# Token routing and parts of the expert layer issued between the edge batches of a graph-attention and mixture-of-experts kernel

## The chip, the cores and the metric

The kernel runs on one NeuronCore of a Trainium2 chip. The metric is the device time of one execution in microseconds (us), the median of several runs. The names in this text: PE is the matrix engine (TensorE), PEld its weight loads, DVE the vector engine, ACT the scalar engine, POOL is GpSimd, SP is SyncE, which only waits and issues DMAs. "L833" is line 833 of the kernel before.

## The reference

6,250 nodes with 256 features, 100,000 edges sorted by destination. The destinations are skewed towards low node numbers: the first 128 nodes have 14,487 of the edges. A graph-attention layer is followed by a layer of 8 experts, both residual:

```python
# graph part, on layernorm(x); 4 heads of 64 features
messages = h_fwd[src] * direction[:, 0:1] + h_rev[src] * direction[:, 1:2]
scores = leaky_relu(einsum('ef,hf->eh', messages, attn[0]), 0.2)
exp_scores = exp(scores - scores.max(axis=0, keepdims=True))
norm = exp_scores / (segment_sum(exp_scores, dst)[dst] + 1e-10)
outs = [segment_sum(messages * norm[:, hd:hd + 1], dst) for hd in range(4)]
# expert part, on layernorm(x + outs); C = ceil(1.25 * T / 8) rows per expert
idx = argmax(softmax(x @ gate_w + gate_b)); prb = that probability
pos = (cumsum(one_hot(idx), axis=0) * one_hot).sum(-1) - 1
kept = pos < C
buf = zeros((E, C, D)).at[idx, pos].set(x, mode='drop')
ybuf = relu(buf @ w1 + b1) @ w2 + b2
y = ybuf[idx, min(pos, C - 1)] * (prb * kept)
```

Everything is float32. The expert layer's hidden width is 1,024.

## The kernel before

`tile_gnn_ffn_kernel` (from L519) works in five stages, each in its own scope of buffers, one after another. (`general_path` above it computes the same for any input; it runs at the end, at L1113, only if a flag `bad_i` says that the assumptions of the fast path do not hold.)

1. **Node table** (L667 to L698). The 49 tiles of 128 nodes, in 7 chunks, are normalised and multiplied by both weight matrices; the table of 136 values per node goes to DRAM as `node_tab`. Then the edge lists are loaded and transposed (L703 to L739), and DVE derives for each group of 768 edges (`GT` = 6 tiles of 128) the first destination and the place of each edge in the group's window of 128 nodes (`local`, L751). SP also writes zeros to `buf` (L793).
2. **Edges** (L811 to L912): 131 groups in 66 batches of two. Per batch: POOL issues 12 indirect gathers from `node_tab` into `gt`, which has four buffers (L831 to L835). DVE forms the messages `m` (L841 to L848), the scores (L851 to L859); ACT takes the exponential (L863); DVE forms the products `v` (L865) and the one-hot matrix `hot` (L870). PE sums each group over its edges into `pv` (L876) and adds the sum carried over from the group before with a matrix `zt` (L885). ACT copies `pv` to `r` (L887, four buffers) and SP stores it into `sums` at a row read from a register (L888 to L890). `m`, `v` and `hot` have three buffers.
3. **Routing** (L946 to L1027): 7 chunks of 7 tiles. `sums` is read back, divided and added to x, normalised, transposed on PE, multiplied by the gate (L966); some 25 small DVE operations turn the gate's values into a slot per token; POOL scatters each tile's rows into `buf` (L1021).
4. **Experts** (L1032 to L1086): for each of the 8 experts the weights are loaded on SP (two buffers), up to 977 rows come on ACT's queue in eight pieces and are transposed (L1058), multiplied with `w1` (L1068), passed through ReLU (L1070), multiplied with `w2` (L1077); DVE adds the bias and SP stores to `ybuf` (L1086).
5. **Combining** (L1091 to L1107): POOL gathers each token's row of `ybuf` (L1097, four buffers), ACT scales it (L1100), DVE clamps and adds, SP stores.

Each engine works its instructions in its queue's order. In the kernel before a scheduler puts the instructions of one scope in order. A later stage starts when what it reads is complete: the routing reads `sums` that the last edge group has written, the experts read `buf` that the last token may have entered, the combining reads `ybuf`.

Of the kernel before, what the change touches and what calls it, by code (L numbers as in the profile page):

```python
# [8 lines left out]
F32 = mybir.dt.float32  # L9
# [5 lines left out]
P = 128  # L15
# [504 lines left out]
def kernel(  # L520
# [24 lines left out]

    nc = tc.nc
# [23 lines left out]
    CHAIN = 16  # L570
    SPREAD = 40.0
    TROWS = N + P - 1
    NSLOT = E * CAP
# [5 lines left out]
    sums = dram.tile([TROWS, ACC], F32, name="sums")  # L579
    buf = dram.tile([NSLOT + NT * P, D], F32, name="buf")  # L580
# [39 lines left out]
    def load_nodes(t, c):  # L620

        r0 = c * CH * P
        if c < NCK - 1:
            nc.sync.dma_start(t, x[r0:r0 + CH * P, :].rearrange("(n p) d -> p n d", p=P))
            return
        nc.vector.memset(t[96:P, CH - 1, :], 0.0)
        r1 = (NT - 1) * P
        nc.sync.dma_start(t[:, :CH - 1, :], x[r0:r1, :].rearrange("(n p) d -> p n d", p=P))
        nc.sync.dma_start(t[:LAST, CH - 1, :], x[r1:N, :])

    def store_nodes(to, t, c):
        r0 = c * CH * P
        if c < NCK - 1:
            nc.sync.dma_start(to[r0:r0 + CH * P, :].rearrange("(n p) d -> p n d", p=P), t)
            return
        r1 = (NT - 1) * P
        nc.sync.dma_start(to[r0:r1, :].rearrange("(n p) d -> p n d", p=P), t[:, :CH - 1, :])
        nc.sync.dma_start(to[r1:N, :], t[:LAST, CH - 1, :])

    def layernorm(pool, h, t):  # L640

        st = pool.tile([P, CH, nc.vector.BN_STATS_DIM], F32, name="ln_st")
        mv = pool.tile([P, CH, nc.vector.BN_AGGR_DIM], F32, name="ln_mv")
        for n in range(CH):
            nc.vector.bn_stats(st[:, n, :], t[:, n, :])
            nc.vector.bn_aggr(mv[:, n, :], st[:, n, :])
        sd = pool.tile([P, CH], F32, name="ln_sd")
        nc.scalar.activation(sd, mv[:, :, 1], AF.Sqrt, bias=eps_t)
        rs = pool.tile([P, CH], F32, name="ln_rs")
        nc.vector.reciprocal(rs, sd)  # L650
        for n in range(CH):
            nc.vector.tensor_scalar(h[:, n, :], t[:, n, :], mv[:, n, 0:1], rs[:, n:n + 1],  # L652
                                    op0=OP.subtract, op1=OP.mult)
# [13 lines left out]
    with tc.tile_pool(name="p1", bufs=2) as p1, \  # L667
# [18 lines left out]
        for c in range(NCK):  # L686
            xt = p1.tile([P, CH, D], F32, name="xt", bufs=3)
            load_nodes(xt, c)
            h = p1.tile([P, CH, D], F32, name="h")
            layernorm(p1, h, xt)  # L690
# [7 lines left out]
            store_nodes(node_tab, nt, c)  # L698
# [8 lines left out]
    dstf = ep.tile([P, EW], F32, name="dstf")  # L707
    ea = ep.tile([P, 2, EW], F32, name="ea")
    with tc.tile_pool(name="pi", bufs=1) as pi, \
# [32 lines left out]
    starts = ep.tile([P, NG + 1], F32, name="starts")  # L742
# [8 lines left out]
    local = ep.tile([P, ET], F32, name="local")  # L751
# [6 lines left out]
    high = ep.tile([P, NG], F32, name="high")  # L758
    nc.vector.tensor_sub(high, starts[:, 1:NG + 1], begin)
    carry_from = ep.tile([P, NG], F32, name="carry_from")  # L760
# [3 lines left out]
    nc.vector.tensor_tensor(carry_from[:, CHAIN:GF], last_tile[:, CHAIN:GF], high[:, CHAIN:GF], OP.is_equal)  # L764

    base_f = ep.tile([1, NG], F32, name="base_f")
    nc.vector.tensor_scalar(base_f, begin[0:1, :], 0.0, float(N - 1), op0=OP.max, op1=OP.min)
    base_i = ep.tile([1, NG], I32, name="base_i")
# [4 lines left out]
    wrong = ep.tile([P, 5], F32, name="wrong")  # L773
    t0 = ep.tile([P, ET], F32, name="t0")
# [13 lines left out]
    nc.vector.memset(wrong[:, 4:5], 1.0)  # L788
    nc.vector.tensor_sub(t0[0:1, CHAIN:GF], high[0:1, CHAIN:GF], last_tile[0:1, CHAIN:GF])
    nc.vector.tensor_reduce(wrong[0:1, 4:5], t0[0:1, CHAIN:GF], AX.X, OP.min)  # L790
    nc.vector.tensor_scalar(wrong[:, 4:5], wrong[:, 4:5], 0.0, None, op0=OP.is_le)

    for r in range(0, NSLOT, 512):  # L793
        k = min(512, NSLOT - r)
        nc.sync.dma_start(buf[r:r + k, :].rearrange("(p n) d -> p (n d)", n=4), zeros[:k // 4, :])

    nc.sync.dma_start(sums[N:TROWS, :], zeros[0:TROWS - N, 0:ACC])


    batches = [list(range(g, min(g + 2, NG))) for g in range(0, NG, 2)]  # L800
    GB = 2 * GT
    gmax = ep.tile([P, len(batches), H], F32, name="gmax")
    shift = ep.tile([P, H], F32, name="shift")
    ZN = 8
# [4 lines left out]


    with tc.tile_pool(name="p2", bufs=3) as p2, \  # L811
            tc.tile_pool(name="ps2", bufs=6, space=bass.MemoryType.PSUM) as ps2:


        fixed = ps2.tile([P, P + H + 2 * (2 + H) * GB], F32, name="fixed", bufs=1)
        nc.vector.tensor_copy(fixed[:, 0:P], lane)
        lane_p, shift_p = fixed[:, 0:P], fixed[:, P:P + H]
        turns = fixed[:, P + H:].rearrange("p (t k j) -> p t k j", t=2, j=GB)

        def over_partitions(to, t):  # L820

            pm = ps2.tile([P, H, P], F32, name="pm", tag="pv")
            for hd in range(H):
                nc.tensor.transpose(pm[:, hd, :], t[:, hd:hd + 1].to_broadcast([P, P]), ident)
            nc.vector.tensor_reduce(to, pm, AX.X, OP.max)

        before = None
        for b, gs in enumerate(batches):
            i0, i1 = gs[0] * GT, min((gs[-1] + 1) * GT, ET)
            n = i1 - i0  # L830
            gt = p2.tile([P, GB, ROW], F32, name="gt", bufs=4)  # L831
            for i in range(i0, i1):
                nc.gpsimd.indirect_dma_start(  # L833
                    out=gt[:, i - i0, :], out_offset=None, in_=node_tab,
                    in_offset=bass.IndirectOffsetOnAxis(ap=srci[:, i:i + 1], axis=0))  # L835
            m = p2.tile([P, GB, MS], F32, name="m")

            fac = turns[:, b % 2, 0:2, :]
# [3 lines left out]
            for g in gs:  # L842
                a0, a1 = g * GT - i0, min((g + 1) * GT, ET) - i0
                k = a1 - a0
                rv = ps2.tile([P, GT, MS], F32, name="rv", bufs=1)
# [10 lines left out]
            if b == 0:  # L856
# [4 lines left out]
            w = fixed[:, P + H + (b % 2 * (2 + H) + 2) * GB:P + H + (b % 2 + 1) * (2 + H) * GB]  # L861
            w = w.rearrange("p (j h) -> p j h", h=H)
            nc.scalar.activation(v[:, :n, H * O:ACC], s, AF.Exp)  # L863
            nc.vector.tensor_copy(w[:, :n, :], v[:, :n, H * O:ACC])  # L864
# [4 lines left out]
            hot = p2.tile([P, GB, P], F32, name="hot")  # L869
            nc.vector.tensor_tensor(hot[:, :n, :], lane_p.unsqueeze(1).to_broadcast([P, n, P]),  # L870
                                    local[:, i0:i1].unsqueeze(2).to_broadcast([P, n, P]), OP.is_equal)
            for g in gs:
                tiles = list(range(g * GT, min((g + 1) * GT, ET)))
                pv = ps2.tile([P, ACC], F32, name="pv")
                for i in tiles:
                    nc.tensor.matmul(pv, hot[:, i - i0, :], v[:, i - i0, :], start=(i == tiles[0]),  # L876
                                     stop=(i == tiles[-1] and before is None))
                if before is not None:
                    k = (g - 1) % ZN
                    z = zt[(g - 1) // ZN % 2]  # L880
                    if k == 0:
                        nz = min(ZN, NG - g)

                        nc.vector.tensor_copy(z[:, 0:nz, 0], carry_from[:, g - 1:g - 1 + nz])
                    nc.tensor.matmul(pv, z[:, k, :], before, start=False, stop=True)  # L885
                r = p2.tile([P, ACC], F32, name="r", bufs=4)
                nc.scalar.copy(r, pv)  # L887
                row = nc.values_load(base_i[0:1, g:g + 1], engines=(mybir.EngineType.SP,), min_val=0,  # L888
                                     max_val=N - 1, skip_runtime_bounds_check_because="clamped to 0..N-1")
                nc.sync.dma_start(sums[bass.ds(row, P), :], r)  # L890
                before = r if g < CHAIN else v[:, tiles[-1] - i0, :]


        pmax = ep.tile([P, H], F32, name="pmax")
        nc.vector.tensor_reduce(pmax, gmax.rearrange("p b h -> p h b"), AX.X, OP.max)
        over = ep.tile([P, H], F32, name="over")
        over_partitions(over, pmax)
        nc.vector.tensor_sub(over, over, shift)
        tiny = const.tile([P, H], F32, name="tiny")
        nc.vector.tensor_scalar(tiny, over, SPREAD, None, op0=OP.min)  # L900
        nc.scalar.activation(tiny, tiny, AF.Exp)
        nc.vector.tensor_scalar(tiny, tiny, 1e-10, None, op0=OP.mult)
        bad = ep.tile([P, 2], F32, name="bad")
        nc.vector.tensor_reduce(bad[:, 0:1], over, AX.X, OP.max)

        nc.vector.tensor_scalar(bad[:, 0:1], bad[:, 0:1], SPREAD, 0.0, op0=OP.is_le, op1=OP.is_equal)
        nc.vector.tensor_reduce(bad[:, 1:2], wrong, AX.X, OP.max)
        nc.vector.tensor_reduce(bad[:, 0:1], bad, AX.X, OP.max)
        pb_ = ps2.tile([P, 1], F32, name="pb_", tag="pv")
        nc.tensor.matmul(pb_, ones, bad[:, 0:1], start=True, stop=True)  # L910
        nc.vector.tensor_copy(bad_i, pb_[0:1, :])
    edges.close()  # L912

    late = fast.enter_context(tc.tile_pool(name="late", bufs=1))
# [225 lines left out]
```

## Time and profile before

| | us |
|---|---|
| median of three runs (2135.83 to 2141.31) | 2136.29 |
| the profiled execution, whole | 2147.85 |
| its span on the core | 2146.1 |
| PE, DVE, POOL, ACT busy in the span | 1146.4, 917.6, 863.3, 224.8 |
| 782 gathers for the edges (L833), mean of one | 0.946 |
| matmuls of the edges (L876, L885), busy | 498.1 + 94.9 |
| first gather at | 100.3 |
| last matmul of the edges' sums at | about 1410 |
| first expert's transposes at | 1585.7 |

Busy time is time in which an engine executes; waiting, branching and issuing a DMA don't count. PE's float32 matmuls appear as two records each, and a weight load goes with each record. The ends of PE's matmuls are modelled. A wait is put down to the instruction whose semaphore came last; "issue" is a wait that nothing in the profile explains, and "remote" one whose release the profile can't place.

### The profile page before, as it was taken

What the parts mean: (1) busy time and instruction counts of PE and PEld (TensorE: products, weight loads), DVE (VectorE), ACT (ScalarE), POOL (GpSimd) and SP (SyncE); (2) the same over time, 40 slices, a digit from 0 to 9 for tenths busy, and PEclk for the clock granted to TensorE, in tenths of its full rate; (3) what the DMA queues carried; (4) which work ended last, traced back from release to release, by engine and by line L of the source; (5) the groups of instructions that cost most, each with busy time, mean ns of one, the idle gap of its engine ahead of it and who ended that gap; (6) DMA issues with size and microseconds to landing.
All of it is one profiled execution on the core that took longest, in us unless ns stands there. A gap on an engine that the chain in (4) does not pass through costs nothing. (4 is left out here: it accounts for less than half of the span.)

```text
span 2146.1 us, 13763 instructions
## 1 busy us (share of the span) xinstructions
PE 1146.4 (53%) x4158; PEld 840.2 (39%) x4158; DVE 917.6 (43%) x1827; ACT 224.8 (10%) x506; POOL 863.3 (40%) x896
## 2 busy tenths in 40 slices
PE   6421446434443454444334444545559999999900
PEld 5310334323232333333223333435436666666600
DVE  7540555544444455644345355657612222221134
ACT  2100000000000000000000000012211111111122
POOL 0176655555555665655556665103410000000065
PEclk9755677766666667766666766765569999999955
DMA  8522222222222222222222222162222222211034
GB/s 262 190 58 52 57 55 55 59 54 53 52 57 58 57 57 54 67 59 53 53 56 57 62 58 55 33 202 74 74 82 77 77 77 77 72 57 43 17 107 138
DMA packets 114150, 158.65 MB, mean 74 GB/s; under 512 B 19762, under 2 KB 94289, under 8 KB 113939
## 3 DMA queue, kind: packets, MB, share of 16 engines
q0 software_dynamic: 29728, 67.35, 13.8%
q1 hardware_dynamic: 66734, 74.20, 10.5%
q10 hardware_dynamic: 17604, 16.13, 2.4%
q8 instruction: 35, 0.57, 0.1%
q14 instruction: 49, 0.39, 0.1%
HBM read 107.80 MB, written 49.80 MB: 73 GB/s over the span
## 5 line engine op out<-in xcount | busy, mean ns | idle before, releaser
L833 POOL DMA_INDIRECT gt<-node_tab,srci x782 | 740.0, 946 | 623.0 <-DVE sc L851 278.7
L876 PE MATMUL pv<-v,hot 128*128 128x260 f32 x1564 | 498.1, 477 | 544.9 <-DVE hot L870 381.2
L876 PEld LDWEIGHTS pv<-v,hot 128*128 128x128 f32 x1564 | 370.3, 241 | 656.2 <-issue 578.5
L864 DVE COPY fixed<-v 128x48 f32<-128x48 f32 x66 | 13.9, 210 | 600.8 <-ACT v L863 393.7
L1097 POOL DMA_INDIRECT yg<-ybuf,to_get x49 | 64.9, 1325 | 484.4 <-issue 477.2
L1077 PE MATMUL py<-w2t,hf 128*128 128x256 f32 (+1 forms) x1024 | 222.3, 379 | 0.0
L865 DVE TENSOR_TENSOR v<-m,fixed 128x3072 f32<-128x3072 f32 x66 | 218.6, 3312 | 4.2
L1068 PE MATMUL ph<-xT,w1t 128*128 128x489 f32 (+1 forms) x512 | 213.9, 576 | 1.1 <-ACT hf L1070 1.0
L1077 PEld LDWEIGHTS py<-w2t,hf 128*128 128x128 f32 (+1 forms) x1024 | 189.6, 185 | 34.2 <-issue 3.5
L1080 DVE TENSOR_TENSOR y<-py,b2b 128x256 f32<-128x256 f32 x64 | 27.1, 424 | 359.1 <-PE py L1077 359.1
L887 ACT COPY r<-pv 128x260 f32<-128x260 f32 x131 | 48.4, 376 | 1053.2 <-issue 481.5
L1068 PEld LDWEIGHTS ph<-xT,w1t 128*128 128x128 f32 x512 | 95.8, 190 | 112.4 <-issue 104.2
L1070 ACT ACTIVATE hf<-ph,b1t 128x489 f32<-128x489 f32 (+1 forms) x128 | 84.4, 670 | 366.9 <-DMA xe<-buf 203.4
L885 PE MATMUL pv<-v,zt 128*128 128x260 f32 x228 | 81.6, 428 | 67.6 <-issue 67.6
L870 DVE TENSOR_TENSOR hot<-fixed,local 128x1536 f32<-128x1536 f32 x66 | 114.1, 1730 | 0.0
L1021 POOL DMA_INDIRECT buf<-h,to_put x49 | 56.2, 1147 | 106.0 <-DVE to_put L1015 66.7
L885 PEld LDWEIGHTS pv<-v,zt 128*128 128x128 f32 x228 | 51.9, 228 | 87.1 <-issue 78.6
L659 PE MATMUL pt<-ident,h 128*128 128x128 f32 x196 | 47.1, 361 | 69.0 <-DVE h L652 29.2
L841 DVE TENSOR_TENSOR gt<-gt,fixed 128x816 f32<-128x816 f32 x66 | 65.5, 993 | 29.0 <-DMA gt<-node_tab,srci 17.4
L848 DVE TENSOR_TENSOR m<-gt,rv 128x408 f32<-128x408 f32 x131 | 75.5, 576 | 4.5
L846 DVE TENSOR_TENSOR rv<-gt,fixed 128x408 f32<-128x408 f32 x131 | 76.1, 581 | 2.2
L885 PE MATMUL pv<-r,zt 128*128 128x260 f32 x32 | 13.3, 506 | 110.4 <-issue 71.9
(171 smaller groups left out, 747.9 us busy)
## 6 DMA issues: line engine op xcount, KB each, us to landing
sums<-r SPq DMA_DIRECT2D x131, 130.0 KB
gt<-node_tab,srci POOLq DMA_INDIRECT x782
w1t<-in_L_ffn_w_dram SPq DMA_DIRECT2D x8, 1024.0 KB
w2t<-in_L_ffn_w_dram SPq DMA_DIRECT2D x8, 1024.0 KB
buf<-zeros SPq DMA_DIRECT2D x15, 512.0 KB
xe<-buf ACTq DMA_DIRECT2D x56, 128.0 KB
ybuf<-y SPq DMA_DIRECT2D x56, 128.0 KB
part<-sums ACTq DMA_DIRECT2D x7, 910.0 KB
```

The costliest lines, as they stand in the source:

```text
L833: nc.gpsimd.indirect_dma_start(out=gt[:, i - i0, :], out_offset=None, in_=node_tab, in_offset=bass.IndirectOffsetOnAxis(ap=srci[:, i:i + 1 ...
L841: nc.vector.tensor_mul(fw, fw, fac[:, 0, :n].unsqueeze(2).to_broadcast([P, n, MS]))
L846: nc.vector.tensor_mul(rv[:, :k, :], gt[:, a0:a1, MS:ROW], fac[:, 1, a0:a1].unsqueeze(2).to_broadcast([P, k, MS]))
L848: nc.vector.tensor_add(m[:, a0:a1, :], fw[:, a0:a1, :], rv[:, :k, :])
L865: nc.vector.tensor_mul(v[:, :n, 0:H * O].rearrange("p n (h o) -> p n h o", h=H), m[:, :n, 0:O].unsqueeze(2).to_broadcast([P, n, H, O]), w[ ...
L870: nc.vector.tensor_tensor(hot[:, :n, :], lane_p.unsqueeze(1).to_broadcast([P, n, P]), local[:, i0:i1].unsqueeze(2).to_broadcast([P, n, P]) ...
L876: nc.tensor.matmul(pv, hot[:, i - i0, :], v[:, i - i0, :], start=(i == tiles[0]), stop=(i == tiles[-1] and before is None))
L885: nc.tensor.matmul(pv, z[:, k, :], before, start=False, stop=True)
L1068: nc.tensor.matmul(ph[:, :b - a], w1t[:, d, f * P:(f + 1) * P], xT[:, d, a:b], start=(d == 0), stop=(d == DC - 1))
L1070: nc.scalar.activation(hf[:, a:b], ph[:, :b - a], AF.Relu, bias=b1t[:, e * FC + f:e * FC + f + 1])
L1077: nc.tensor.matmul(py[:k, :], hid[f][:, a:b], w2t[:, f, :], start=(f == 0), stop=(f == FC - 1))
L1097: nc.gpsimd.indirect_dma_start(out=yg, out_offset=None, in_=ybuf, in_offset=bass.IndirectOffsetOnAxis(ap=to_get[:, j:j + 1], axis=0))
```

## The change

The change rewrites stages 2 to 5 into one scope with `manual_schedule()`: each engine gets its instructions in the order in which the program issues them. What was done stage by stage is cut into steps (generators that yield their estimated PE cost), and a loop over the edge batches issues them between the batches' own work.

- The edge groups that lie in the first tile alone (`HEAD`, here 17 of 131) come last, and their windows go to a table `sums_b` of their own. So tiles 1 to 48 are complete, chunk by chunk (now 4 tiles, 12 chunks, and tile 0 as the thirteenth), while later batches still run.
- A batch is split: `messages(b)` now also makes `hot`; then comes the first `windows` of batch b-1, a share of expert steps, `products(b)`, the second `windows` of b-1, and expert steps again. `gt` has three buffers and is gathered three batches ahead; `m`, `v`, `hot` have two, `pv` two, and routing and experts share three further PSUM buffers.
- Routing of a chunk starts when its last group's batch is past. Up to three of its steps are issued per iteration. The softmax's added constant is taken from the running maximum (`term`), once per chunk. x after the graph layer goes to DRAM (`x2_d`) instead of staying on chip.
- The scatters into `buf` are put between the gathers on POOL's queue, one after every second gather, an iteration later.
- The expert layer is done in five passes of 128, 256, 256, 256 and 128 rows per expert (`TOT` = 1,024 rows instead of 977), each over all 8 experts; every pass loads all the weights again. A pass can start when its tiles' rows are scattered (after tiles 8, 20, 32, 44 and the end). Per iteration the experts get `SHARE` = 8.6 units less the cost of routing. Rows of an expert come in one load on SP; the copy after the transposes is on ACT.
- What is left of the passes is issued after the last batch, with the combining of earlier passes' tiles in pairs between its steps, and the rest of the combining behind it. The flags for `bad_i`, with new ones for the added assumptions, are formed at the very end.
- Zeros are written to `buf` and `ybuf` in the first iterations, by SP.

The core of the diff (steps of unchanged arithmetic left out):

```diff
+    PASS = (128, 256, 256, 256, 128)
+    CK = 4
+    chunks = [list(range(t, min(t + CK, NT))) for t in range(1, NT, CK)] + [[0]]
+    LASTS = (8, 20, 32, 44, 0)
...
-    batches = [list(range(g, min(g + 2, NG))) for g in range(0, NG, 2)]
+    order = [list(range(g, min(g + 2, NG))) for g in range(HEAD, NG, 2)]
+    order += [list(range(g, min(g + 2, HEAD))) for g in range(0, HEAD, 2)]
+    NB = len(order)
...
+        def gathers(b):
+            gts[b] = p2.tile([P, GB, ROW], F32, name="gt", bufs=3)
+            for i in range(i0, i1):
+                nc.gpsimd.indirect_dma_start(
+                    out=gts[b][:, i - i0, :], out_offset=None, in_=node_tab,
+                    in_offset=bass.IndirectOffsetOnAxis(ap=srci[:, i:i + 1], axis=0))
+                if (i - i0) % 2 == 1 and pool_work:
+                    pool_work.pop(0)()
...
+        def fetch_rows(p, e):
+            x_loads.append(nc.sync.dma_start(xe, buf[a:a + S, :].rearrange("(p j) d -> p j d", j=J)))
...
+        def experts(p):
+            S = PASS[p]
+            J = S // P
+            FB = 512 // S
+            ws = {0: fetch_weights(0)}
+            xs = {0: fetch_rows(p, 0)}
+            yield 0.0
+            xT = columns(p, xs.pop(0))
+            yield 0.43 * J
+            for e in range(E):
+                w1t, w2t = ws.pop(e)
+                if e + 1 < E:
+                    ws[e + 1] = fetch_weights(e + 1)
+                    xs[e + 1] = fetch_rows(p, e + 1)
+                for f0 in range(0, FC, FB):
...
+                    yield 0.85 * FB * J
+                if e + 1 < E:
+                    xT = columns(p, xs.pop(e + 1))
+                    yield 0.43 * J
...
+                    if j + 1 < J:
+                        yield 3.4
...
+                yield 3.4
...
+        for b in range(3):
+            gathers(b)
+        for b in range(NB + 1):
+            for p in [p for p, at in started.items() if b >= at]:
+                passes.append(experts(p))
+                del started[p]
+            if b < NSLOT // 512:
+                clear(buf, 512 * b)
+                clear(ybuf, 512 * b)
+            if b < NB:
+                messages(b)
+            if b:
+                windows(b - 1, order[b - 1][0])
+            step_experts(SHARE / 2)
+            if b < NB:
+                products(b)
+            if b and len(order[b - 1]) > 1:
+                windows(b - 1, order[b - 1][1])
+            step_experts(SHARE / 2)
+            while next_c < len(chunks) and done_at[next_c] < b:
+                routing.append(routes_of(next_c))
+                next_c += 1
+            step_routing(3)
+            pool_work.extend(held)
+            held = todo[:]
+            del todo[:]
+            if b + 3 < NB:
+                gathers(b + 3)
+            if not pool_work and not held and not todo:
+                for p in wait_pass:
+                    started[p] = b + 2
+                del wait_pass[:]
+        while routing:
+            step_routing(1)
...
+        for q, gen in enumerate(passes):
+            per = max(1, -(-len(work) // 20))
+            for cost in gen:
+                for _ in range(per if cost > 1 else 0):
+                    if work:
+                        combine(work.pop(0))
+            work += fetch[left + q - 1]
+        for tiles in work + fetch[NP - 1]:
+            combine(tiles)
```

## The prediction

> **What bounds the kernel now.** I read the windows first, one per stage, cut at the first gather (100 us), the end of the edge stage (1411), the first expert (1580) and the last expert's store (2044). The columns are the stretch, its length, then the busy time (and instructions) of PE, PE's weight loads, DVE, ACT and POOL, the granted clock, the DMA share and GB/s.
>
> ```profile
> 100.00:1411.00 1311.00, 566.38 (x1834) 430.74 (x1834) 617.37 (x837) 60.86 (x198) 739.95 (x782) 0.68 0.24 55
> 1411.00:1580.00 169.00, 72.44 (x324) 64.85 (x324) 103.75 (x504) 35.15 (x74) 56.48 (x51) 0.51 0.36 116
> 1580.00:2044.00 464.00, 452.01 (x1665) 300.34 (x1665) 91.46 (x225) 84.40 (x128) 0.00 (x0) 0.99 0.20 65
> 2044.00:2146.00 102.00, 0.00 (x0) 0.00 (x0) 43.48 (x28) 24.67 (x49) 64.91 (x49) 0.50 0.41 127
> ```
>
> The stages stand one after another. In the experts PE is full (452 of 464 us at clock 0.99) and everything else idle. In routing and in combining nothing is full; they are latency. In the edge stage, 61% of the span, no engine is full either, so I asked for its waits, from 200 to 1380 us (idle time in total, times, longest):
>
> ```profile
> DVE fixed L864 <- ACT v L863: 390.5, 37, 63.3
> PE pv L876 <- DVE hot L870: 376.0, 41, 25.0
> POOL gt L833 <- DVE sc L851: 278.7, 20, 18.7
> ACT r L887 <- remote: 393.0, 27, 36.7
> ```
>
> DVE waits for ACT, ACT for PE, PE for DVE, POOL for DVE: a ring, so the timeline has to say who is really late. Columns: start, duration, engine, line, operation, count, [idle before].
>
> ```profile
> 777.10 0.60 PE L885 MATMUL pv<-v,zt 128*128 128x260 f32 x2
> ...
> 789.57 0.38 PE L876 MATMUL pv<-v,hot 128*128 128x260 f32 x1 [1.72 <-issue]
> 790.98 0.29 PEld L876 LDWEIGHTS pv<-v,hot 128*128 128x128 f32 x1 [2.62 <-issue]
> 792.37 0.59 PE L876 MATMUL pv<-v,hot 128*128 128x260 f32 x1 [2.42 <-issue]
> ...
> 809.93 0.38 ACT L887 COPY r<-pv 128x260 f32<-128x260 f32 x1 [33.26 <-remote]
> ```
>
> The copy of a group whose last matmul is shown at 777.1 starts at 809.93, and meanwhile TensorE starts one instruction in about 1.4 us, where a weight load and its matmul otherwise go by in 0.22 us together. So PE itself crawls: 12 pairs of 2 x 1.4 us are 33.6 us, the length of the hole. This comes back every three batches. POOL tells when: it gathers in runs of 36 (45 us, 1.25 us each), then waits about 15 us for a free buffer:
>
> ```profile
> 805.17 0.95 POOL L833 DMA_INDIRECT gt<-node_tab,srci  x1 [0.30 <-issue]
> 822.46 0.94 POOL L833 DMA_INDIRECT gt<-node_tab,srci  x1 [16.34 <-DVE sc L851]
> ```
>
> The crawl begins some 14 us into a run and is over about 6 us after its last gather (806.1 to 812.1). When the gathers are all done, at the stage's end, a batch takes 10.2 us (two L865 products, one batch apart):
>
> ```profile
> 1374.67 3.35 DVE L865 TENSOR_TENSOR v<-m,fixed 128x3072 f32<-128x3072 f32 x1
> 1384.85 3.35 DVE L865 TENSOR_TENSOR v<-m,fixed 128x3072 f32<-128x3072 f32 x1
> ```
>
> With gathers it takes 1311/66 = 19.9 us. The edge stage is bound by a cycle of 60 us: 45 us of gathers plus 15 us until DVE frees a buffer, with PE useful for only some 26 us of it (60 less 776 to 810). What the profile does not tell is why PE crawls.
>
> **What the Trainium skill says.** "Perfetto Trace Analysis", Tensor Engine Instruction: a matmul's reported end is an estimate, not an observation. The trace agrees: the end at 777.7 and the release at 809.9 cannot both be read as work, so I date PE by ACT's copies. "SBUF — State Buffer", SBUF: two separate sides: PE never waits on another engine's port there. The trace gives no support to that here: PE is slow only while gathers are issued. "TensorE: Matmul & The Clock Gate", What's actually happening: half clock after an idle window. It agrees (0.43 us a pair cold, 0.22 warm; clock 0.68 in the edge stage) but gives a factor of 2, not 13. "DMA: Bandwidth & Descriptors", Issuing engines are not separate DMA queues: all issuers share 16 engines; with a share of 0.24 in the edge stage there is room for moved weights.
>
> **The change, part by part.** Base: the profiled 2147.85 us (span 2146.1); it lies 0.5% above the median 2136.29, and I take the 0.5% off at the end.
>
> *Experts.* A matmul record of 256 columns costs 27.64/128 = 0.216 us. One expert in a pass of 256 rows: 32 records for the first layer, 32 for the second, 0.86 for transposes: 14.5 us; of 128 rows, 7.2. Five passes: 58 + 3 x 116 + 58 = 464, as now. When they are issued is the loop's own bookkeeping. With HEAD = 17, tile 8 is complete at batch 19, so pass 0 starts at iteration 25, pass 1 at 40, pass 2 at 51, 3 at 60. Each iteration grants 8.6 of the program's cost units less routing's (4.8 a chunk of four tiles): 38 iterations x 8.6 - 48 = 279 units. A pass of 680 units in all is 464 us by the trace (the first layer is entered at twice its cost), so 190 us are issued between batches and 274 after the last. *Gain 464 - 274 = 190.*
>
> *Routing.* 169 us now. Afterwards 12 of 13 chunks lie in the loop. DVE: 104 us now, plus six more chunks of 24 small operations (0.19 us) = 27, plus 13 running maxima of about 2 (L895 0.62, L825 0.69, four small ones) = 26: 157 us over 54 iterations, 2.9 each, against 10.5 idle (19.9 less 9.4 busy). Hidden; without cover it would cost the 157. Only tile 0 stays after the last batch, at the head of each queue: two DMA hops of about 2.5 us (the last scatter landed after 2.43), some 60 DVE operations, two table loads of 1.28: 35 us. *Gain 134.*
>
> *Combining.* 102 us now, 2.08 a tile. The pairs are spread over later passes, each a pass late, so tiles 33 to 48 and tile 0, 17 tiles, remain at the end: 35 us. The flag chain, now early, comes last: 6. *Gain 61.*
>
> *Weights.* 16.8 MB are read five times. At 262 GB/s (first slice) an expert's 2.1 MB take 8.0 us: hidden under 14.5, not under 7.2 in the last pass: *loss 6*. Clearing and set-up: 3 us more before, as the 15 stores of zeros go into the loop on SP.
>
> *The edge loop.* PE's useful 26 us a cycle carried 72 of 84 pairs, 12 crawled. Now each cycle also needs 3 x 190/38 = 15 us of expert matmuls and 2 of routing: 84 x 0.22 + 17 = 36 us, 10 more than there are. 38/3 = 12.7 cycles: *loss 127*, if matmuls wait for the crawl's end. Two terms I can't date: 49 scatters of 1.27 on POOL's queue lengthen the runs (0 to 62 loss); and DVE now computes the next batch's messages before the products, with two v and hot buffers, so up to 8 us of a crawl is used in each of 22 cycles (0 to 176 gain). I take one against the other, as the third gt buffer less leaves POOL less reserve.
>
> *New waits.* SP is one queue: an expert's row load waits for the scatters issued before it, which sit behind gathers in POOL's queue. Behind it wait the stores of r (three buffers), hence ACT's copies and the next exponential. No row shows it; bounds: 0 (scatters drained before a pass starts, only later chunks matter) to 24 loads x 20 us = 480. I take 0, since a crawl covers it.
>
> *Sum:* 190 + 134 + 61 - 6 - 3 - 127 = 249. 2147.85 - 249 = 1899; times 0.995: **1890**.
>
> **Rivals.**
> A, *PE no longer crawls* (runs of gathers longer than 14 us do not form, because DVE's fuller batches pace POOL): the edges are then bound by gathers, 66 x 15 + 62 = 1052, with fill and drain 1110 instead of 1311; with no loss of 127, 2147.85 - 201 - 376 = 1571, about 1560. For: bursts need three free buffers. Against: POOL is still the fullest queue.
> B, slower: *expert matmuls are caught in the crawl.* Each caught pair costs 2.8 instead of 0.22. Some 900 pairs are issued in the loop; without the 127, 376/2.6 = 145 caught pairs, one in six, undo the gain. PE takes work in order, so whatever is at its head when a run is 14 us old crawls. At one in four: 225 x 2.6 = 585, less 376: 2350. For: 34 of 60 us crawl. Against: the run ends when buffers are full, whatever PE does.
> C, *SP's queue holds the stores* at half its bound, 240 us: 2130, no change.
> D, the change doesn't do what it says: its guards fail and the general path runs. Worked out from the reference's inputs, all hold (first edge of group 17 goes to node 103, below 128; no expert is two passes late). Nothing.
>
> **Numbers.** Forecast 0.48 (its own range 1760 to 2030), A 0.27, B 0.19, C 0.06. The range 1540 to 2170 leaves out most of B and a little of A. This kernel's measurement tells 0.3% from no change. Faster 0.78 (forecast, A, half of C), same 0.03 (the rest of C), slower 0.19.
>
> **What would show it.** Right: after the last gather about 35 us of tile 0, then 274 us of full PE, 40 us of tail; an edge loop near 1440 with runs of gathers and ACT copies 30 us late. A: no single matmuls 1.4 us apart. B: singles on the experts' lines. C: SP's row load waiting for buf. Wrong altogether: PE idle after the loop, from weights or rows that come late.

## The result, and the profile after

The changed kernel takes 2299.41 us (median of 4 runs, 2294.7 to 2301.22); the kernel before, beside it, 2138.8. The ratio is 1.073, with an interval of 1.068 to 1.079: slower by 7%, where the prediction had 1890 us and faster. The profiled execution has a span of 2297.5 us.

Its stages, cut at the first gather, the last copy of `r`, the last token's slot and the last expert's output; columns as in the windows of before:

```profile
102.20:1727.60 1625.40, 840.98 (x3229) 681.77 (x3230) 795.87 (x1545) 165.01 (x436) 787.90 (x830) 0.72 0.32 97
1727.60:1752.50 24.90, 12.70 (x53) 10.50 (x52) 9.79 (x53) 7.00 (x15) 0.99 (x1) 0.73 0.44 138
1752.50:2235.00 482.50, 314.22 (x1378) 267.13 (x1376) 72.28 (x144) 89.88 (x230) 30.96 (x32) 0.82 0.41 137
2235.00:2297.50 62.50, 1.70 (x6) 1.22 (x6) 22.12 (x53) 8.73 (x18) 16.85 (x17) 0.54 0.37 111
```

Two stages went wrong. The edge loop takes 1625 us (1311 before, forecast 1438). After it the rest of the experts takes 483 us (forecast 274), although the loop took in what was forecast: 963 of the 2304 matmul records of L1208 and L1220 (42%, some 194 of 464 us) lie before its end. In that stretch PE is busy for 314 us only, at a clock of 0.82 instead of 0.99.

Where the loop's time goes shows in the groups of DVE in the loop. The columns are line, engine, operation, out<-in, shapes, times; busy us and mean ns; then DVE's idle time ahead of the group and what ended it. First the lines of the edges' own work:

```profile
L981 DVE TENSOR_TENSOR hot<-fixed,local 128x1536 f32<-128x1536 f32 (+1 forms) x66 | 114.3, 1731 | 205.4 <-remote 160.0 <-issue 42.7 <-PE pv L1008 2.7
...
L990 DVE COPY fixed<-v 128x48 f32<-128x48 f32 (+1 forms) x66 | 14.0, 211 | 125.3 <-ACT v L979 104.5 <-issue 16.4 <-DVE hot L981 0.5
...
L1225 DVE TENSOR_TENSOR y<-py,b2b 128x512 f32<-128x512 f32 (+1 forms) x17 | 9.6, 564 | 153.3 <-PE py L1220 146.7 <-remote 6.0 <-issue 0.6
...
L920 DVE TENSOR_REDUCE over_s<-pm 128x4 f32<-128x512 f32 x12 | 8.3, 692 | 72.5 <-remote 59.5 <-PE pm L919 8.2 <-PE ph L1208 3.9
...
L1084 DVE TENSOR_TENSOR lg<-pl,gb 128x32 f32<-128x32 f32 x12 | 2.3, 192 | 96.8 <-PE pl L1081 69.1 <-remote 22.7 <-issue 5.0
...
L1054 DVE TENSOR_SCALAR den<-part 128x16 f32<-128x16 f32 x12 | 2.2, 188 | 74.6 <-DMA part<-sums 74.6
```

The lower four are new: an expert's sum, the running maximum, the gate's values, the sums read back. They work for 22 us and wait for 397: for PE, and for a DMA. What DVE has to do next for the edges stands behind each of them in its queue.

The crawl (PE starting one instruction in 1.4 us, as the prediction describes it) is still there. A copy of `r` comes 34 us after the one before, just as a run of gathers ends:

```profile
308.81 1.76 DVE L981 TENSOR_TENSOR hot<-fixed,local 128x1536 f32<-128x1536 f32 x1 [18.55 <-remote]
...
313.15 0.94 POOL L943 DMA_INDIRECT gt<-node_tab,srci  x1 [0.30 <-issue]
314.46 0.38 ACT L1020 COPY r<-pv 128x260 f32<-128x260 f32 x1 [33.88 <-issue]
```

Holes of over 10 us between the recorded end of a PE group and its signal add up to 686 us before (22 holes) and 417 after (19): from 590 us on most runs of gathers are at most 24 long, where they were 36. So the crawl got less, and the loop longer all the same.

### The profile page after: what moved, and what is told of

It is laid out like the page before. It is cut to its first block, busy times and chain, and to the rows that moved or that the text cites. A ratio compares the mean times of both kernels' runs of the same rounds, so it can differ in the third digit from the quotient of the medians.

```text
span 2297.5 us, 16040 instructions
## 1 busy us (share of the span) xinstructions
PE 1226.4 (53%) x5000; PEld 1005.3 (44%) x5000; DVE 969.4 (42%) x2074; ACT 290.3 (13%) x755; POOL 838.9 (37%) x896
## 4 chain that ended last, share of the span: by engine, by line
PE 26%; DVE 24%; issue 21%; DMA 16%; another core or an unknown queue 8%; SPq 2%; ACT 2%; POOL 1%; DVEq 0%; ACTq 0%; POOLq 0%
PE py L1220 10%; DMA xe<-buf 8%; PE pv L1008 6%; DVE v L991 4%; PE ph L1208 4%; DMA part<-sums 3%; DMA xr<-x_d 2%; DVE hot L981 2%; DVE m L966 2%; DVE rv L964 2%; PE pv L1017 2%; DVE gt L959 2%; PE pn L716 1%; PE px L1183 1%
## 5 line engine op out<-in xcount | busy, mean ns | idle before, releaser
L1008 PE MATMUL pv<-v,hot 128*128 128x260 f32 x1564 | 464.5, 457 | 307.4 <-issue 141.4
L1220 PE MATMUL py<-w2t,hf 128*128 128x256 f32 x1024 | 290.3, 445 | 80.5 <-ACT hf L1211 56.9
L1208 PE MATMUL ph<-xT,w1t 128*128 128x256 f32 (+1 forms) x1280 | 268.9, 368 | 50.9 <-issue 27.8
L1220 PEld LDWEIGHTS py<-w2t,hf 128*128 128x128 f32 x1024 | 230.7, 230 | 129.8 <-ACT hf L1211 60.6
L1208 PEld LDWEIGHTS ph<-xT,w1t 128*128 128x128 f32 x1280 | 230.4, 212 | 81.1 <-issue 27.4
L991 DVE TENSOR_TENSOR v<-m,fixed 128x3072 f32<-128x3072 f32 (+1 forms) x66 | 218.7, 3314 | 6.3 <-issue 0.5
L981 DVE TENSOR_TENSOR hot<-fixed,local 128x1536 f32<-128x1536 f32 (+1 forms) x66 | 114.3, 1731 | 205.4 <-remote 160.0
L1211 ACT ACTIVATE hf<-ph,b1t 128x256 f32<-128x256 f32 (+1 forms) x320 | 116.1, 431 | 350.6 <-PE ph L1208 279.3
L1183 PE MATMUL px<-ident,xe 128*128 128x128 f32 x128 | 29.8, 361 | 209.6 <-DMA xe<-buf 209.6
L959 DVE TENSOR_TENSOR gt<-gt,fixed 128x816 f32<-128x816 f32 (+1 forms) x66 | 65.6, 993 | 36.5 <-DMA gt<-node_tab,srci 26.7
L990 DVE COPY fixed<-v 128x48 f32<-128x48 f32 (+1 forms) x66 | 14.0, 211 | 125.3 <-ACT v L979 104.5
```

What stands on the lines that cost most here:

```text
L959: nc.vector.tensor_mul(fw, fw, fac[:, 0, :n].unsqueeze(2).to_broadcast([P, n, MS]))
L991: nc.vector.tensor_mul(v[:, :n, 0:H * O].rearrange("p n (h o) -> p n h o", h=H), m[:, :n, 0:O].unsqueeze(2).to_broadcast([P, n, H, O]), w[ ...
L1183: nc.tensor.transpose(px[:, d, j * P:(j + 1) * P], xe[:, j, d * P:(d + 1) * P], ident)
L1208: nc.tensor.matmul(ph[:, f - f0, :], w1t[:, d, f * P:(f + 1) * P], xT[:, d, :], start=(d == 0), stop=(d == DC - 1))
L1211: nc.scalar.activation(hf[:, f, :], ph[:, f - f0, :], AF.Relu, bias=b1t[:, e * FC + f:e * FC + f + 1])
L1220: nc.tensor.matmul(py[:, j, :], hf[:, f, j * P:(j + 1) * P], w2t[:, f, :], start=(f == 0), stop=(f == FC - 1))
```

## Experiments 1 and 2: the loop taken apart

Theory: what is new in the loop is not hidden. Rival: the loop's own rearrangement (order of tiles, fewer buffers) is to blame. One kernel leaves the experts until after the loop, the other the routing as well.

```diff
-        SHARE = 8.6
+        SHARE = 0.0
 ...
-            work += fetch[left + q - 1]
+            work += fetch[left + q - 1] if left + q else []
# second kernel, besides:
-            step_routing(3)
```

> Routing stays between the edge batches, the five expert passes all come after the last batch. The changed kernel's edge loop (first gather to last window copy) takes 1625 us, 1311 before the change. Theory 1, routing's short chains stand in DVE's and PE's order between two batches and are not hidden: with the experts gone the loop is still far over 1311, 1420 to 1500. Theory 2, the expert matmuls lengthen the loop, each about its own length or more: the loop falls to 1311 to 1360. In either case all 464 us of expert work stand at the end, stretched as the changed kernel's tail is (483 us for what would be 264 at full clock, a factor of 1.8): some 830 us for all passes, and a total of 2370 to 2480 under theory 1 and 2280 to 2340 under theory 2.

> Neither routing nor experts between the batches: the loop has only the new order of tiles, the new order of each engine's work and the smaller numbers of buffers (three gathered tiles instead of four, two of the messages, products and one-hot tiles instead of three). It shows what the loop itself costs. If that rearrangement is to blame, the loop takes well over 1311 us (1400 or more); if it is neutral, as the first 26 batches suggest (585 us in both kernels), 1290 to 1340. The rest of the time (routing in one buffer after the loop) is not compared.

In the second kernel, and in experiments 5, 7, 10 and 12 to 18 except 16, POOL also clears one column beside each scatter that is left for after the loop. The experiments ran on four chips (1 to 4, 5 to 8, 9 to 12, 13 to 18), on which the kernel before takes 2147, 2145, 2157 and 1829 us. Ratios are with the kernel before on the same chip; the length of a loop is that of one profiled execution. The loops with nothing between and with the routing:

```profile
101.30:1391.70 1290.40, 554.03 (x1830) 431.68 (x1830) 612.84 (x829) 58.94 (x198) 738.01 (x782) 0.70 0.24 67
```

```profile
102.60:1626.40 1523.80, 651.67 (x2214) 519.03 (x2214) 771.72 (x1494) 110.77 (x282) 786.83 (x830) 0.67 0.26 74
```

Measured: with nothing between, the loop takes 1290 us; with the routing 1524, more than either theory had; with both 1625. (Whole: 2563.52 us for nothing between, 2511.8 for the routing, above the 2370 to 2480 expected.) So the rearrangement changes little (21 us less, as much as the kernel before differs between these chips), routing costs 234, the experts 101. The rival falls. The 234 hold the routing's 48 scatters on POOL's queue too, which were not tried by themselves.

I then added up DVE's time in the loop, instruction by instruction from the traces, as work and as idle time ahead of an instruction, by what the instruction belongs to (us; neighbouring instructions overlap a little and count twice there, so the rows exceed the loops by 1 to 3%):

| loop with | length | edges: work, waits | routing: work, waits | experts: work, waits |
|---|---|---|---|---|
| nothing between | 1290 | 625, 670 | | |
| routing | 1524 | 625, 467 | 177, 280 | |
| routing and experts | 1625 | 625, 388 | 177, 286 | 26, 154 |
| pause, nothing between (experiment 5) | 1182 | 625, 567 | | |
| pause, routing (experiment 9) | 1257 | 637, 280 | 190, 186 | |

Routing put 457 us into DVE's queue. The edges' own waits fell by only 203 of their 670 us; the rest came on top. More than half of the 457 is waiting, which the prediction had not costed. One chunk of the kernel with routing alone shows both (timeline of DVE):

```profile
831.39 0.37 DVE L925 TENSOR_REDUCE top_s<-gmax 128x4 f32<-128x124 f32 x1
...
840.76 0.17 DVE L1054 TENSOR_SCALAR den<-part 128x16 f32<-128x16 f32 x1 [6.51 <-DMA part<-sums]
...
848.51 0.18 DVE L957 COPY fixed<-ea 128x24 f32<-128x24 f32 x1
```

From 831.4 to 848.5 DVE does nothing for the edges, and the next batch's first instruction (L957) stands behind it. In the kernel with nothing between, the idle time lies as follows:

```profile
L981 DVE TENSOR_TENSOR hot<-fixed,local 128x1536 f32<-128x1536 f32 (+1 forms) x66 | 114.4, 1733 | 396.4 <-remote 278.0 <-issue 100.1 <-PE pv L1008 18.3
...
L959 DVE TENSOR_TENSOR gt<-gt,fixed 128x816 f32<-128x816 f32 (+1 forms) x66 | 65.6, 994 | 39.1 <-DMA gt<-node_tab,srci 28.6 <-DVE fixed L957 7.0 <-issue 3.4
...
L990 DVE COPY fixed<-v 128x48 f32<-128x48 f32 (+1 forms) x66 | 13.9, 211 | 212.5 <-ACT v L979 198.7 <-issue 9.4 <-DVE hot L981 1.3
```

609 of 670 us are spent in front of two instructions, L981 and L990, in pieces of up to 27 us; the signals of PE have 23 holes in this loop. What is issued behind these two instructions cannot use that time.

## Experiments 3, 4 and 8: what stretches the experts after the loop

Before the change the rows came on ACT's queue; now they follow the next expert's weights on SP's. SP's issues and the PE instruction that waits, in the changed kernel:

```profile
1942.04 0.38 SPq L1165 DMA_DIRECT2D w1t<-in_L_ffn_w_dram  x1
1942.48 0.48 SPq L1167 DMA_DIRECT2D w2t<-in_L_ffn_w_dram  x1
1943.01 0.58 SPq L1175 DMA_DIRECT2D xe<-buf  x1
...
1950.70 1.12 PE L1183 MATMUL px<-ident,xe 128*128 128x128 f32 x4 [7.53 <-DMA xe<-buf]
```

The rows (256 KB) arrive 7.7 us after their issue, behind 2 MB of weights, and PE needs them in the middle of an expert, not at its end. The Trainium skill ("DMA: Bandwidth & Descriptors", Two DMAs through the same engine are not ordered) says that within one queue of one DMA engine descriptors start in order, though they may overlap. These 7.7 us agree with it, and the prediction had left it out. Experiment 3 asks for them first:

```diff
-                    ws[e + 1] = fetch_weights(e + 1)
                     xs[e + 1] = fetch_rows(p, e + 1)
+                    ws[e + 1] = fetch_weights(e + 1)
# and the same for a pass's first expert
```

> An expert's rows are asked for ahead of the next weights instead of behind them. Theory 1, the rows (256 KB) come 4 to 8 us late because 2.1 MB of weights are ahead of them on the same queue: the 20 waits of TensorE for rows after the last batch (146 us) mostly go, the clock comes up from 0.82, the expert stretch falls from 483 to 320 to 370 us and the whole to about 2150 to 2190. Rival, the rows wait for something else (scatters, the stores of y on SP's queue, the weights' own buffers): within 20 us of 2299.

Experiment 4 combines no token between the passes (`range(per if cost > 1 else 0)` becomes `range(0)`); experiment 8 does both edits.

> No token is combined between the passes after the loop; all 49 are combined at the end. Theory 1, the combining holds the stores and the row loads through the shared table of expert outputs and SP's one queue, and costs more than it hides: the expert stretch falls by 60 us or more from 483, against some 70 us more of combining at the end (102 us for 49 tiles before the change, 62 after it), total 2280 to 2310. Rival, the combining is hidden and the expert stretch is set by rows and weights alone: stretch 465 to 483, total 2320 to 2350.

> Rows ahead of weights, and all combining after the last pass. With weights ahead, moving the combining to the end took 59 us off the expert stretch and put 76 us on the end. If the two costs are separate, the stretch falls from 367 to some 310 and the total stays at 2166 to 2190. If the combining only cost because it held up the same row loads, the stretch stays at 350 to 367 and the total is 2230 to 2245.

Measured: rows first 2166.05 us, 1.008 of before (1.005 to 1.012); combining last 2319.39, 1.080 (1.076 to 1.084); both 2164.79, 1.010 (1.007 to 1.013). The stretch with rows first, then with both:

```profile
1735.00:2102.30 367.30, 283.85 (x1379) 246.52 (x1377) 72.74 (x147) 88.66 (x231) 31.18 (x32) 0.88 0.53 180
```

```profile
1728.50:2022.00 293.50, 273.97 (x1387) 241.97 (x1386) 39.78 (x92) 75.47 (x200) 0.99 (x1) 0.97 0.53 183
2022.00:2159.00 137.00, 1.70 (x6) 1.22 (x6) 55.78 (x117) 25.09 (x50) 49.86 (x49) 0.51 0.47 142
```

483 us become 367 and 294, at clocks of 0.82, 0.88 and 0.97; PE's waits for rows fall from 145.9 us to 52.1 in the first step. So of the 209 us over the forecast 116 are late rows, 73 the combining, and 20 are left. In the other order the shares differ a little: with the rows still late, combining last takes 59 us off (483 to 424), and rows first then 130. Combining between the passes hides nothing: its 73 us come back as 75 at the end, and the total doesn't move (2166 and 2165). By what the combining holds the experts up was not tried.

## Experiments 5, 6, 9 and 11: is it the crawl?

The prediction could not say why PE crawls, only that it does from some 14 us into a run of gathers. If the run matters, breaking it should help. POOL overwrites the tile twice before each batch's gathers:

```diff
             gts[b] = p2.tile([P, GB, ROW], F32, name="gt", bufs=3)
+            for _ in range(2):
+                nc.gpsimd.memset(gts[b], 0.0)
```

Experiment 5 does this in the loop with nothing between, 9 with the routing between, 6 in the whole kernel with rows first. Experiment 11 breaks the runs in the kernel before, by a copy that needs the last gathered row:

```diff
             gt = p2.tile([P, GB, ROW], F32, name="gt", bufs=4)
+            if b:
+                nc.gpsimd.tensor_copy(gt[:, :, 0:1], last.to_broadcast([P, GB, 1]))
+            last = gt[:, n - 1:n, 0:1]
```

> As the loop with neither routing nor experts (1290 us), but GpSimd overwrites the tile twice, some 3 us, before each batch's twelve gathers, so that no run of gathers is longer than 15 us. Theory 1, TensorE crawls once a run has lasted some 14 us, and any pause of 3 us ends the run: the holes of 20 to 40 us in TensorE's signals (23 of them in the loop) vanish and the loop is paced by GpSimd alone, 66 x (15 + 3 to 4) = 1190 to 1260 us. Rival, the crawl follows the number of gathers under way or the waiting of the ring itself, not the length of a run: the holes stay and the loop grows by the pauses, to 1290 + 100 to 200.

> Rows ahead of weights (2166 us, its loop 1607) and the same pause before each batch's gathers, with routing and experts between the batches. If the crawl is what takes TensorE and VectorE away in one block per run, the routing's 160 us of VectorE and the experts' matmuls find room and the loop falls to 1250 to 1400, the whole to 1820 to 1960. If the routing's chains in the order of the engines are what costs (each chunk some 19 us wherever it stands), the loop stays at 1550 or more.

> With the pause before each batch's gathers, routing between the batches and no experts there. Without the pause routing lengthened the loop by 234 us (1290 to 1524), of which 159 are VectorE's own work. With the pause and nothing between, the loop takes 1182. If VectorE's idle time was there all along but lay in one block behind an instruction that waits for the crawling TensorE, it is now spread (8.5 of 17.9 us in each batch) and routing costs well under its own 159: a loop of 1210 to 1290. If the chains themselves cost (a wait for the sums and one for TensorE in each of 12 chunks), it stays near 234: 1380 to 1420.

> The kernel before the change, with one edit: GpSimd copies a column of the last gathered row of a batch into the next batch's tile, so the next run of gathers starts only when the last row has landed, some 2 to 3 us later. Theory, the crawl comes from the length of a run alone: the 22 holes of some 30 us go, the edge stage falls from 1311 to 66 x 17.5 to 18.5 = 1155 to 1220 and the whole to 2000 to 2060. Rival, the crawl or its cure belongs to the changed loop's order: edge stage 1311 or more and 2140 to 2300.

Measured: the loop with nothing between falls from 1290 to 1182 us, 66 x 17.9, paced by POOL alone (a little under the 1190 to 1260 expected); its 23 holes are gone. Part of its timeline:

```profile
642.00 2.99 POOL L943 MEMSET gt<- 128x1632 f32 x2
...
645.26 0.95 POOL L945 DMA_INDIRECT gt<-node_tab,srci  x1 [0.27 <-POOL gt L943]
...
659.01 0.94 POOL L945 DMA_INDIRECT gt<-node_tab,srci  x1 [0.30 <-issue]
...
659.94 2.99 POOL L943 MEMSET gt<- 128x1632 f32 x2
661.96 1.00 DVE L961 TENSOR_TENSOR gt<-gt,fixed 128x816 f32<-128x816 f32 x1 [8.55 <-POOL gt L943]
```

Most of DVE's idle time now lies in every batch, ahead of its first large instruction (8.55 us here), and not in blocks in front of L981 and L990. With it routing costs 75 us instead of 234, and the table's last row shows 287 of 567 us used. The loop with the pause and the routing:

```profile
104.20:1361.00 1256.80, 626.13 (x2214) 506.38 (x2214) 787.95 (x1493) 110.40 (x282) 984.95 (x960) 0.70 0.32 89
```

The whole kernel with rows first falls from 2166.05 to 1953.47 us, 0.910 of before (0.907 to 0.914). The kernel before with its runs broken takes 2063.71, 0.957 (0.955 to 0.959), its edge loop 1227 instead of 1311, with no hole left (both just above the ranges expected, 2060 and 1220).

With work between the batches the pause does not remove every hole: 12 of 10 to 17 us remain with the routing (163 us), 7 with routing and experts (114 us, one of 39). In the loop with the routing the scatters lengthen 12 of the runs to some 20 us, and 7 of the 12 holes begin in these.

## Experiments 7, 10 and 12: are the waits on the path?

Experiment 7 takes one of the new waits away: a chunk's loads are issued an iteration before DVE needs them (rows first too). Experiment 10 adds the pause; 12 grants 14 instead of 8.6 units of expert work per iteration besides.

```diff
+            yield 0.0
+            yield 0.0
+            yield 0.0
             tiny = tinies[:, c, :]
```

> Rows ahead of weights (2166 us, its loop 1607), and a chunk's two loads are issued one iteration before VectorE needs them. In the loop without experts VectorE waited 52 us for the sums between 400 and 1390 us (10 times), with them 64 us. Theory, these waits stand on the path and are part of the 234 us that routing costs: the loop falls by 40 to 70, the whole to 2100 to 2130. Rival, they are covered by TensorE's holes: no change, within 10 us of 2166.

> Rows ahead of weights, the pause, and a chunk's loads an iteration early, all three. The kernel with the first two takes 1953 us, its loop 1392. The early loads gave 53 us of loop without the pause. If those waits are still on the path: loop 1330 to 1360, whole 1890 to 1925. If the pause has given VectorE enough slack to take them: 1940 to 1960.

> As the kernel with all three edits, with 14 instead of 8.6 units of expert work granted in each iteration. If TensorE's free time between the batches is real without the crawl (5.6 of 17.9 us used by the edges), some 300 instead of 200 us of expert work go into the loop, the loop grows by less than half of that and the whole falls by 40 to 80 us. If the loop is already bound by the order of the engines, it grows by as much as the tail shrinks: within 20 us of it.

Measured: 2117.55 us with the loads early, 0.988 of before (0.985 to 0.992), its loop 1554 instead of 1607. DVE's wait for the sums (69 us there) is gone, those for the running maximum are 27 shorter, and 47 us come back as a wait of L669 for ACT: routing's waits fall by 49 in all (282 to 233), the loop by 53. (Some 7 us of that are 34 expert records fewer in it.) With the pause 1915.3 us, 0.888 of before (0.886 to 0.890), the loop 1348 instead of 1392: the waits are on the path there too. More expert work in the loop (1347 instead of 929 of the 2304 matmul records) brought nothing: 1930.96 us; the loop grew by 114 us, what is after it shrank by 94. PE's free time was not what limited it.

## Experiments 13 to 18: another chip

Experiment 13 pauses before every second batch (`range(2 if b % 2 == 0 else 0)` in experiment 5), 14 half as long (`range(1)`); 15 is experiment 10 with the half pause.

> As the loop with nothing between and a pause before each batch (1182 us, no hole in TensorE's signals), with the pause before every second batch only: runs of 24 gathers, 30 us. If the age of a run decides (about 14 us), each run has a hole of 12 to 20 us at its end, some 30 holes, however much VectorE has to do. If any regular pause is enough (the gathers under way come to a limit only in long runs of 36), there are hardly any holes and the loop is paced by GpSimd at 33 x 33 = 1090 us.

> The same loop with a pause of one overwrite (1.5 us and the waits around it) instead of two before each batch. If what must happen is only that the stream of gathers is broken, there are no holes and the loop takes 66 x 16.4 = 1080 to 1110 us. If the gathers issued have to drain first, a pause this short doesn't reset it: holes of 15 us and more come back, 1150 to 1300.

> Rows ahead of weights, loads an iteration early, and the half pause. With the full pause 1915 us, its loop 1348. If the half pause cures the crawl as well, up to 1.5 us a batch come off where GpSimd sets the pace, which is the first 25 batches above all: 1850 to 1900. If not: 1950 to 2100.

These were to tell whether the age of a run decides or the draining of the gathers. They ran on a chip on which the kernel before takes 1828.6 us instead of some 2140, and no trace from it has a hole of 10 us in PE's signals: not with runs of 24 gathers (loop 1086 us), not with the half pause, where all 782 gathers follow each other with gaps of at most some 2 us (loop 1086). So they tell nothing of that question. The kernel with all three edits and the half pause takes 1787.3 us there, below its expected ranges, which were for the other chips: 0.976 of before (0.973 to 0.979). The change itself ran on that chip too, and experiments 13 and 15 once more.

> The changed kernel once more, on whichever chip it gets. On the chips of the earlier runs the kernel before takes 2136 to 2157 us and this one 2299; on the chip of the last three runs the kernel before took 1829 us and no trace there has a hole in TensorE's signals, in gathers of any length. If the kernel before takes some 2140 us here, this one takes 2290 to 2310. If it takes some 1830, the crawl is not there: theory 1, the crawl is what makes routing dear (75 us instead of 234), and the change's ratio to before falls from 1.073 to 1.00 to 1.04, since the late rows and the combining still cost their 190 us; rival, routing costs in any case and the ratio stays at 1.07 or rises.

Measured: before 1827.71, the change 1947.94, ratio 1.065 (1.063 to 1.068); the repeats gave 1086.6 us for the loop and 1786.46. That is far from the 1.00 to 1.04 of theory 1 and near the rival's 1.07: the change costs 120 us more than the kernel before, where it cost 161 with the crawl. Both kernels gain by the crawl's absence, the kernel before 311 us and the change 351. The groups of DVE in the change's loop (1275 us):

```profile
L981 DVE TENSOR_TENSOR hot<-fixed,local 128x1536 f32<-128x1536 f32 (+1 forms) x66 | 114.2, 1730 | 2.5 <-PE pv L1008 2.5
...
L959 DVE TENSOR_TENSOR gt<-gt,fixed 128x816 f32<-128x816 f32 (+1 forms) x66 | 65.6, 993 | 105.3 <-DMA gt<-node_tab,srci 101.0 <-DVE fixed L957 1.6
...
L1225 DVE TENSOR_TENSOR y<-py,b2b 128x512 f32<-128x512 f32 (+1 forms) x17 | 9.6, 564 | 113.2 <-PE py L1220 113.1
...
L920 DVE TENSOR_REDUCE over_s<-pm 128x4 f32<-128x512 f32 x12 | 8.3, 692 | 24.9 <-PE pm L919 24.9
...
L1084 DVE TENSOR_TENSOR lg<-pl,gb 128x32 f32<-128x32 f32 x12 | 2.3, 192 | 77.4 <-PE pl L1081 77.4
...
L1054 DVE TENSOR_SCALAR den<-part 128x16 f32<-128x16 f32 x12 | 2.2, 187 | 73.3 <-DMA part<-sums 73.3
```

L981 no longer waits, but routing's and the experts' instructions wait for 214 and 114 us all the same. The wait for the running maximum has shrunk most (L920, from 73 us in the first trace of the change to 25): there the crawl had been part of the new waits. DVE's queue holds 830 us of work and 328 of their waits: 1158 us, against 66 x 15.0 = 990 us of gathers.

## Why the prediction was wrong

*The account.* Forecast 1899 in the profiled execution, 2297.5 came:

| step | forecast | measured | difference |
|---|---|---|---|
| loop, rearrangement | 0 | -21 | -21 |
| loop, routing | 0, hidden | +234 | +234 |
| loop, experts | +127 | +101 | -26 |
| tile 0 after the loop | 35 | 25 | -10 |
| experts after the loop | 274 + 6 | 483 | +203 |
| combining at the end | 41 | 62 | +21 |

Together +401: 2300, within 3 us of what came. (One expert's sum in the prediction comes to 14.7 us and not 14.5; that is 1% of the 464 and changes nothing.)

*The step that failed most* is routing: "157 us over 54 iterations, 2.9 each, against 10.5 idle ... Hidden; without cover it would cost the 157." The 157 was right (DVE's busy time in the loop went from 613 to 772 us, 159). Two things were not. The 10.5 us were an average: they lay in blocks of up to 27 us, in front of instructions of the edges, where nothing issued later can run. And the new instructions wait themselves, 280 us in all, for the sums, for the running maximum's transposes and for the gate's matmul; I costed their work and no wait. The pause speaks for the first (75 instead of 234), though it also slows POOL from 15 to 17.9 us a batch, which by itself leaves room to hide work. The second was shown by the early loads (53 us of loop for 49 of waits), and the change is slower on the chip without the crawl too, where routing still waits for 214 us. How much of the 234 is blocks and how much waits is not settled.

*Weights* failed next: "hidden under 14.5". The transfer is hidden; what was put behind it on the same queue is not, and is due half an expert earlier. 116 us, with a clock that falls from 0.97 to 0.82 across all such gaps. I had named this case as what would show the forecast wrong altogether, and gave it no price; the term *New waits*, taken at 0, looked for the rows behind the scatters and not behind the weights.

*Combining* failed: "gain 61". It costs 73 between the passes and 62 after them, against 102.

*The edge loop's 127* was near (101), but partly by luck: it stood for PE lacking 10 us in each cycle of 60. Most of those cycles were gone, and DVE's waits for the experts' sums (154 us) took their place; they are 114 us without the crawl too. *The experts in the loop* (190 us) were right, and *tile 0* (35) nearly.

*Rivals.* A got its premise in part (shorter runs, fewer holes) and not its time: what then sets the pace is, as far as the table tells, the order of DVE's queue and not the gathers. B has the right sign by the wrong mechanism: only 3 of 19 holes begin at the experts' lines. C named as its sign that SP's row load waits for `buf`; SP's waits in the changed kernel have none at that load (L1175), and the swap of two lines, which leaves the scatters where they are, moved the loop by only 18 us. That the stores of `r` are held up was not tried by itself.

*Open:* why PE crawls on some chips while gathers are issued, and whether the age of a run or its draining decides. On the chip without it the loop was not split into routing and experts, and the kernel before was not profiled.

## What to carry to other kernels

Idle time of an engine that works in order is not a store to be spent: look up in front of which instruction it lies, because only what is issued ahead of that instruction can use it. Price an inserted chain by its waits as well as its work; issue its loads a whole iteration before the instruction that reads them (53 us here); the same for what it needs of other engines suggests itself, but was not tried. On a shared queue put the small load that is due first ahead of the large one (133 us here). The best kernel here (rows first, loads early, runs broken) takes 0.888 of before where there is a crawl. Part of this is the broken runs alone: against the kernel before with broken runs, on the same chip, it is 1915.3 to 2063.71, or 0.928.

## What the hardware showed

On one chip a pause of 3.3 us on POOL after every 12 indirect gathers (14.7 us) removed all of PE's 23 holes from a loop with nothing else in it; on another, one copy per batch left none of the 22 that the kernel before had shown, and took 4.3% off it. With other work between the batches some holes remained. On yet another chip the kernel before runs 15% faster (1828 for some 2140 us). None of the traces from there has a hole of 10 us, not even the change's, whose first 360 gathers follow each other with no gap of 2.5 us: one chip's profile is not every chip's.
